# One seed and one gate step per two blocks in a fused attention and expert loop

## The chip, the cores and the metric

The kernel runs on one core of one Trainium2 chip. Its time is the device time of one execution in microseconds (us); the figure for the kernel is the median of several runs. The core has five engines that run side by side, each in the order of its own queue: PE (matrix products and transposes), DVE (vector work), ACT (activation functions, copies), POOL (elementwise work, and the issue of some transfers) and SP (the issue of most transfers). They wait for each other through semaphores.

## What is computed

Two layers on x of 2 x 1024 tokens of width 128 in 32-bit floats. Each layer has two attention-like parts, each followed by a feed-forward part. The change touches the second half of the second layer:

```python
def _L1_attn_b_ref(x, w_qkv, b_qkv, w_proj, b_proj):      # 16 heads of 8
    ...
    dp = jnp.einsum('bhqd,bhkd->bhqk', q, k) * SCALE
    attn = jax.nn.softmax(dp, axis=1)                     # over the heads
    w_avg = jnp.einsum('bhqk,bhkd->bhqd', attn, v)
    ...
    return w_avg @ w_proj + b_proj

def _L1_ffn_ref(hidden_states, Wg, Wu, Wd):               # 8 experts, 128 -> 512 -> 128
    def expert_step(acc, w):
        wg, wu, wd = w
        h = jax.nn.silu(x @ wg) * (x @ wu)
        return (acc + h @ wd, None)
    ...
```

The softmax runs over the 16 heads, not over the keys: for each pair of a query and a key, the exponentials of the 16 scores are divided by their sum. The expert part is applied once before this attention and once after it, so expert work on some tokens can stand beside attention on others.

## The kernel before

The order of all instructions around the change is written out by hand: in `heads_and_experts` each engine gets its instructions in the order in which the Python code records them.

The loop runs over 128 blocks (2 batches x 8 blocks of 128 queries x 8 blocks of 128 keys). One step `i` of it works on several blocks at once, as a pipeline:

- block `i + 1`: `products` (PE, L1237) writes the 16 heads' scores into `h_s`, four banks of PSUM with one buffer. `maxima` (DVE, L1248) takes the maximum over the heads, `exponentials` subtracts it (DVE, L1254) into one of seven `h_e` buffers and applies Exp in two halves (ACT, L1257).
- The sum over 16 heads starts with two transfers: `lower` (SP, L1262) copies heads 0 to 7 into `h_e2`, `upper` (POOL's queue, L1265) adds heads 8 to 15 onto them.
- `denominators` (PE, L1271) adds the remaining 8 by transposes that accumulate in the PSUM tile `h_pd`, which has one buffer. Two blocks share it: even steps and the odd steps after them form a pair. Each pair takes 16 transposes, 8 in a call, where a call has four heads of both blocks.
- In the next even step `inverse` (DVE, L1283) takes the reciprocal of 128 x 256 sums, `turned` (PE, L1288) transposes it back, `evacuated` (ACT, L1292) copies it to `h_r`.
- `normalize` (POOL, L1296) multiplies the block's exponentials by it, four steps after their own; `weigh` (PE, L1301) multiplies by the values one step later. After 8 key blocks the sum is copied (ACT, L1421), its bank set to zero (L1422) and projected (PE, L1383), and `x_res` gets the result (DVE, L1398).

Between these, `ExpertStream` does expert work. A unit is 256 tokens x one expert x 128 of the 512 inner columns. `products` (L1060) makes the gate and up products of a unit in one bank, `e_pgu`, of which there are two; `gates` applies Silu (ACT, L1067), `multiply` multiplies (DVE, L1075), `outputs` makes the Wd products (PE, L1085), at most two units a step. A step takes two units, or one where another use of a bank (`turn` or a side step on PE) comes in. Side steps (`aside`) are the norms and projections of tokens to come. `alone` runs expert work without a block: before the loop until few units are left, and after it for the rest; then `experts_ffn` handles the last 512 tokens.

On ACT, Silu, Exp, Ln and Sqrt need tables; the build puts a load (ACT_TABLE_LOAD) before an activation whose table is not the one that was loaded last. In the loop each step has Silu first and then the next block's Exp.

Of the kernel before, what the change touches and what calls it, by code (L numbers as in the profile page):

```python
# [9 lines left out]
F32 = mybir.dt.float32  # L10
BF16 = mybir.dt.bfloat16
AF = mybir.ActivationFunctionType
ALU = mybir.AluOpType
# [6 lines left out]
P = 128  # L20
# [988 lines left out]
class ExpertStream:  # L1009
# [6 lines left out]

    def __init__(self, g, w, work, ps, sums, zero):
        self.g, self.w, self.work, self.ps, self.sums, self.zero = g, w, work, ps, sums, zero
        self.units, self.fresh, self.gated, self.ready, self.summed, self.done = [], [], [], [], [], []


# [40 lines left out]

    def gates(self):
        nc = self.g.nc
        for chunk, e, fc, pgu in self.fresh:
            sg = self.work.tile([P, 2 * P], F32, name="e_sg", bufs=4)
            nc.scalar.activation(sg, pgu[:, 0, :], AF.Silu)  # L1067
            self.gated.append((chunk, e, fc, pgu, sg))
        self.fresh = []

    def multiply(self):
        nc = self.g.nc
        for chunk, e, fc, pgu, sg in self.gated:
            h = self.work.tile([P, 2 * P], F32, name="e_h", bufs=4)
            nc.vector.tensor_mul(h, sg, pgu[:, 1, :])  # L1075
            self.ready.append((chunk, e, fc, h))
        self.gated = []

    def outputs(self):

# [26 lines left out]
    turned = None  # L1107

    def add(self):

        if self.turned:
            chunk, pt = self.turned
            self.turned = None
            xt = self.tokens(chunk)
            self.g.nc.vector.tensor_add(xt, xt, pt[:, 0:2, :])

# [11 lines left out]
def heads_and_experts(g, w, first, second):  # L1128

    nc, tc = g.nc, g.tc  # L1130
    J, K, HD, H = 4, 4, 8, 16
    scale = HD**-0.5
    with ExitStack() as es:
        pool = lambda name, bufs, **kw: es.enter_context(tc.tile_pool(name=name, bufs=bufs, **kw))
        one = pool("h_one", 1)
        seq = pool("h_seq", 2)
        work = pool("h_work", 2)
        ework = pool("e_work", 2)
        ps_s = pool("h_ps_s", 1, space=PSUM)
        ps_d = pool("h_ps_d", 1, space=PSUM)  # L1140
# [5 lines left out]

        zero = one.tile([P, 1], F32, name="h_zero")
        nc.vector.memset(zero, 0.0)
        held = ps_o.tile([P, 4 * P], F32, name="h_po")
        sums, po, proj = held[:, 0 : 2 * P], held[:, 2 * P : 3 * P], held[:, 3 * P :]  # L1150

# [13 lines left out]
        ex = ExpertStream(g, w, ework, ps_e, sums, zero)  # L1165
# [60 lines left out]
        def spread(b):  # L1226
            v = vs[b].rearrange("p t (j k d) -> p (t j) k d", j=J, k=K)
            for k in range(K):
                nc.scalar.copy(vz[:, :, k, k, :], v[:, :, k, :])
# [34 lines left out]
        def upper(e2, e):  # L1264
            nc.gpsimd.dma_start(out=e2, in_=e[:, 8:16, :], accum_op=ALU.add)  # L1265

        def denominators(pd, pair, half):

            for k in range(4 * half, 4 * half + 4):
                for t in range(2):  # L1270
                    nc.tensor.matmul(  # L1271
                        pd[:, t, :],
                        pair[:, t, k, :],
                        g.ident,
                        start=(k == 0 and t == 0),
                        stop=(k == 7),
                        is_transpose=True,
                        skip_group_check=True,
                    )

        def inverse(pd):
            rT = work.tile([P, 2, P], F32, name="h_rT")
            nc.vector.reciprocal(rT, pd[:, 0:2, :])  # L1283
            return rT

        def turned(pd, rT):
            for t in range(2):
                nc.tensor.transpose(pd[:, 2 + t, :], rT[:, t, :], g.ident)  # L1288

        def evacuated(pd):  # L1290
            r = work.tile([P, 2, P], F32, name="h_r")
            nc.scalar.copy(r, pd[:, 2:4, :])  # L1292
            return r

        def normalize(e, r):
            nc.gpsimd.tensor_mul(e, e, r.unsqueeze(1).to_broadcast([P, H, P]))  # L1296
# [14 lines left out]

        side = [(0, 28 if k else 16, ex.opening(c)) for k, c in enumerate(first[1:])]
        side += [(0, 64, preparation(1, 0))]
        side += [(2 * c + 2, 16 if c else 28, ex.opening(c)) for c in second]
        side.insert(len(first) + 1, (0, 24, preparation(1, 1)))
        finished, current, head, ex.unopened = 0, None, None, len(first)

        def aside(place):  # L1320

            nonlocal current, head
            while True:
                if head is None:
                    if current is None:
                        if not side or side[0][0] > finished or len(ex.units) > side[0][1]:
                            return False
                        current = side.pop(0)[2]
                    head = next(current, None)
                    if head is None:  # L1330
                        current = None
                        continue
                break
            if head[0] != place:
                return False
            step, head = head[1], None
            step()
            return True
# [17 lines left out]
        n = len(blocks)  # L1356
        with tc.manual_schedule(engines=ALL):
            nc.scalar.copy(held, zero.to_broadcast([P, 4 * P]))
            for _, step in ex.opening(first[0]):
                step()  # L1360
            for half in range(2):
                for place, step in preparation(0, half):
                    step()
                    if place != "act":
                        alone()

            while len(ex.units) + 32 * ex.unopened > 76:
                alone()
            spread(0)
            e_, pairs, d_, r_ = {}, {}, {}, {}  # L1370


            oT = resting = None
            for i in range(-1, n + 7):
                now, resting, oT = resting, oT, None
                if i + 1 < n:
                    heads = products(*blocks[i + 1])
                even = i % 2 == 0
                due = even and 0 <= i - 4 < n
                if due:  # L1380
                    rT = inverse(d_[i - 4])
                if now is not None:
                    nc.tensor.matmul(proj, now, w["w_proj2"], start=False, stop=True, skip_group_check=True)  # L1383
                if resting is None:
                    ex.outputs()
                ex.multiply()
                if due:
                    turned(d_[i - 4], rT)
                    r_[i - 4] = evacuated(d_.pop(i - 4))
                ex.products(1 if ex.turn() or aside("pe") else 2)  # L1390
                if resting is not None:
                    ex.outputs()
                if i + 1 < n:
                    m = maxima(heads)
                ex.add()
                if now is not None:
                    xt = g.x[:, finished, :]
                    nc.vector.tensor_add(xt, xt, proj)  # L1398
                    finished += 1
                aside("act")  # L1400
                ex.gates()
                if i + 1 < n:
                    e_[i + 1] = exponentials(heads, m)
                    if not even:
                        pairs[i + 1] = work.tile([P, 2, 8, P], F32, name="h_e2")
                    lower(pairs[i + 1 - even][:, int(even)], e_[i + 1])
                aside("dve")
                pair = i - 2 if even else i - 3
                if not even and 0 <= pair < n:
                    denominators(d_[pair], pairs.pop(pair), 1)  # L1410
                if 0 <= i - 4 < n:
                    normalize(e_[i - 4], r_[i - 4 - i % 2][:, i % 2, :])
                if 0 <= i < n:
                    upper(pairs[i - i % 2][:, i % 2], e_[i])
                aside("pool")
                if 0 <= i - 5 < n:
                    b, qb, kb = blocks[i - 5]
                    weigh(kb, e_.pop(i - 5))
                    if kb == TPB - 1:
                        oT = work.tile([P, P], F32, name="h_oT")  # L1420
                        nc.scalar.copy(oT, po)  # L1421
                        nc.scalar.copy(held[:, 2 * P :], zero.to_broadcast([P, 2 * P]))  # L1422
                        if qb == TPB - 1 and b + 1 < B:
                            spread(b + 1)

                if even and 0 <= pair < n:
                    d_[pair] = ps_d.tile([P, 4, P], F32, name="h_pd")
                    denominators(d_[pair], pairs[pair], 0)
            while ex.busy() or side or current:
                alone()  # L1430

# [221 lines left out]
```

## Time and profile before

| | |
|---|---|
| timed runs (us) | 2206.4, 2212.57, 2213.07; median 2212.57 |
| the profiled execution (us) | 2201.0, its span 2199.3 |
| granted clock of PE, mean | 0.943 |
| busy over the span: PE, DVE, ACT, POOL | 85%, 75%, 60%, 40% |
| first and last maximum of the loop start at (us) | 1186.1 and 2040.4 |
| table loads in the whole span | 372, 1.283 us each |

The profile names each group of instructions by line, engine, operation, and what is written from what; then how many there are, their busy time, the mean of one in ns, and how long the engine stood idle just before them and what ended that. A matrix product in 32-bit floats counts as two instructions in it. The share of busy time is a mean over stages with different limits, so the loop is read by itself, from 1186 to 2047 us; after it come about 152 us of expert work.

### The profile page before, as it was taken

To read this page: it belongs to the slowest core of one execution; us is meant where nothing else is said; L and a number is where in the kernel's file an instruction comes from. 1 tells how busy PE (TensorE), PEld (TensorE's weight loads), DVE (VectorE), ACT (ScalarE), POOL (GpSimd) and SP (SyncE) were. 2 spreads that over 40 slices of the span, in tenths; PEclk is the share of its full clock that TensorE was granted. 3 is DMA by queue.
4 is the path that set the end of the run, shared out by engine and by line. 5 is a ranking of instruction groups with operands and counts; after the bars stand their busy time and mean duration, and the time that the engine had idled before them with its cause. 6 is when DMAs were issued, how large, how long until landed. Compare 5 with 4: busy or idle time off the path is not lost. (4 is left out here: it accounts for less than half of the span.)

```text
span 2199.3 us, 33893 instructions
## 1 busy us (share of the span) xinstructions
PE 1876.8 (85%) x13632; PEld 1068.8 (49%) x13632; DVE 1656.2 (75%) x1955; ACT 1324.5 (60%) x1762; POOL 870.1 (40%) x432
## 2 busy tenths in 40 slices
PE   7669888889967758898688899999888999998999
PEld 4223243333334323334455566666566666666754
DVE  5976867898774699894424989889888989998422
ACT  1026512276633666763544888888888888888422
POOL 0013400063401000000100778777877878887600
PEclk9989979979988979999899999999999999999999
DMA  4000000197623287530001656665655666666200
GB/s 91 1 1 1 1 1 0 49 228 165 157 71 99 57 201 174 136 82 0 1 1 48 154 153 159 155 161 148 160 152 155 165 154 159 168 159 154 68 5 5
DMA packets 73789, 220.01 MB, mean 100 GB/s; under 512 B 9184, under 2 KB 19872, under 8 KB 73504
## 3 DMA queue, kind: packets, MB, share of 16 engines
q1 hardware_dynamic: 54736, 149.40, 23.3%
q0 software_dynamic: 18432, 67.12, 16.0%
q8 instruction: 107, 1.75, 0.3%
q10 hardware_dynamic: 464, 1.33, 0.3%
q14 instruction: 50, 0.41, 0.1%
HBM read 78.35 MB, written 5.24 MB: 38 GB/s over the span
## 5 line engine op out<-in xcount | busy, mean ns | idle before, releaser
L1296 POOL TENSOR_TENSOR h_e<-h_e,h_r 128x2048 f32<-128x2048 f32 x128 | 599.8, 4687 | 109.6 <-issue 100.0
L1248 DVE TENSOR_REDUCE h_m<-h_s 128x128 f32<-128x2048 f32 x128 | 292.7, 2287 | 71.4 <-PE h_s L1237 71.4
L1254 DVE TENSOR_TENSOR h_e<-h_s,h_m 128x2048 f32<-128x2048 f32 x128 | 293.2, 2290 | 9.6 <-DVE h_m L1248 0.4
L1257 ACT ACTIVATE h_e<-h_e 128x1024 f32<-128x1024 f32 x256 | 256.5, 1049 | 23.0 <-DVE h_e L1254 19.4
L1067 ACT ACT_TABLE_LOAD x134 | 171.9, 1283 | 71.6 <-PE e_pgu L1060 70.5
L385 POOL TENSOR_SCALAR_AFFINE_SELECT a_pT<-a_pT 128x256 f32<-128x256 f32 x120 | 128.5, 1092 | 203.2 <-ACT a_pT L382 200.5
L1060 PE MATMUL e_pgu<-e_uT,Wg 128*128 128x256 f32 x640 | 199.8, 395 | 4.4 <-ACT h_qz L1204 2.3
L1075 DVE TENSOR_TENSOR e_h<-e_sg,e_pgu 128x256 f32<-128x256 f32 x320 | 119.6, 402 | 107.7 <-ACT e_sg L1067 103.9
L287 DVE TENSOR_REDUCE a_nm<-a_s 128x2 f32<-128x1024 f32 (+7 forms) x144 | 167.9, 1217 | 38.3 <-PE a_s L278 26.8
L1060 PE MATMUL e_pgu<-e_uT,Wu 128*128 128x256 f32 x640 | 193.8, 385 | 0.0
L1237 PE MATMUL h_s<-h_qz,h_kT 32*128 32x512 f32 x1024 | 153.5, 668 | 46.0 <-DVE h_e L1254 43.2
L1085 PE MATMUL h_po<-e_h,Wd 128*128 128x256 f32 x640 | 188.7, 412 | 4.0 <-DVE e_h L1075 2.3
L1271 PE MATMUL h_pd<-ident,h_e 128*128 128x128 f32 x1024 | 144.9, 279 | 40.8 <-DMA h_e<-h_e 40.7
L1265 POOL DMA_DIRECT2D h_e<-h_e x128 | 119.5, 933 | 140.8 <-DVE h_m L1248 67.7
L382 ACT ACTIVATE a_pT<-a_st 128x1024 f32<-128x1024 f32 (+3 forms) x176 | 129.9, 791 | 65.4 <-PE a_st L368 62.6
L1067 ACT ACTIVATE e_sg<-e_pgu 128x256 f32<-128x256 f32 x320 | 111.5, 382 | 91.6 <-PE e_pgu L1060 76.3
L1257 ACT ACT_TABLE_LOAD x128 | 164.2, 1283 | 2.3
L1085 PEld LDWEIGHTS h_po<-e_h,Wd 128*128 128x128 f32 x640 | 112.8, 196 | 105.6 <-issue 78.9
L800 DVE TENSOR_TENSOR_SCAN s_h<-s_a,s_h 128x1024 f32<-128x1024 f32 x64 | 148.7, 2323 | 17.9 <-ACT s_a L768 14.1
L269 PE MATMUL a_s<-a_latT,a_qT 32*128 32x512 f32 (+3 forms) x768 | 117.0, 583 | 42.0 <-DVE a_nm L287 40.0
L1271 PEld LDWEIGHTS h_pd<-ident,h_e 128*128 128x128 f32 x1024 | 116.7, 142 | 66.7 <-DMA h_e<-h_e 47.0
L1301 PE MATMUL h_po<-h_e,h_vz 128*32 128x128 f32 x4096 | 138.4, 276 | 7.3 <-DVE x_res L1398 6.1
(293 smaller groups left out, 3118.2 us busy)
## 6 DMA issues: line engine op xcount, KB each, us to landing
h_e<-h_e SPq DMA_DIRECT2D x128, 512.0 KB, 4.6
h_e<-h_e POOLq DMA_DIRECT2D x128, 512.0 KB, 5.4
s_a<-s_steps SPq DMA_DIRECT2D x64, 512.0 KB, 5.1
s_h<-s_steps SPq DMA_DIRECT2D x64, 512.0 KB, 6.5
s_steps<-s_gate SPq DMA_DIRECT2D x8, 256.0 KB, 2.0
Wg<-in_Wg_dram SPq DMA_DIRECT2D x8, 256.0 KB, 5.9
Wu<-in_Wu_dram SPq DMA_DIRECT2D x8, 256.0 KB, 5.9
Wd<-in_Wd_dram SPq DMA_DIRECT2D x8, 256.0 KB, 6.0
```

The costliest lines, as they stand in the source:

```text
L287: nc.vector.tensor_reduce(nm[:, half, i, h : h + together], s[:, :, :n], AX.X, ALU.max, negate=True)
L800: nc.vector.tensor_tensor_scan(h, a, h, 0.0, ALU.mult, ALU.add)
L1060: nc.tensor.matmul(pgu[:, k, :], w[name][:, e, f], uT, start=True, stop=True)
L1067: nc.scalar.activation(sg, pgu[:, 0, :], AF.Silu)
L1085: nc.tensor.matmul(self.sums, self.w["Wd"][:, e, fc, :], h, start=False, stop=last, skip_group_check=True)
L1237: nc.tensor.matmul(s[:, j, :].rearrange("p (k q) -> p k q", k=K), kTs[b][quad, bass.ts(kb, P)], qzs[b][qb // 4][quad, :, bass.ts(qb % 4, P ...
L1248: nc.vector.tensor_reduce(m, heads.rearrange("p h q -> p q h"), AX.X, ALU.max)
L1254: nc.vector.tensor_sub(e, heads, m.unsqueeze(1).to_broadcast([P, H, P]))
L1257: nc.scalar.activation(eh, eh, AF.Exp, scale=scale)
L1271: nc.tensor.matmul(pd[:, t, :], pair[:, t, k, :], g.ident, start=(k == 0 and t == 0), stop=(k == 7), is_transpose=True, skip_group_check=True,
L1296: nc.gpsimd.tensor_mul(e, e, r.unsqueeze(1).to_broadcast([P, H, P]))
L1301: nc.tensor.matmul(po[32 * j : 32 * j + 32, :], vz[:, kb * J + j, k].rearrange("p a d -> p (a d)"), a[:, 4 * j + k, :], start=False, stop= ...
```

## The change

The blocks of the loop are taken two at a time in three ways.

- Gates: odd steps make four units' gate products, two units to a bank (`rise`), and apply Silu to a bank at a time (`open_gates`). The even step after them makes the up products into banks of their own (`follow_up`), and the next odd step multiplies (`multiply_pairs`).
- Inverse: in odd steps, behind the second block's transposes, `seed` takes Ln of the sums and Exp of its negative on ACT. In the even step `refined` does one Newton step on DVE, which gives the negated inverse; `evacuated` multiplies by -1 where it copied.
- `denominators` takes one block per call, all 8 heads: the first block in the even step (now ahead of `weigh`), the second in the odd step.

In addition `log_and_exp` applies Ln to one element behind the gates, and a side step that prepares the second batch waits until its tokens' sums are recorded. The core of the diff:

```diff
+    def rise(self, banks):
+        for _ in range(banks):
+            pair, self.units = self.units[:2], self.units[2:]
+            if pair:
+                self.risen.append((pair, self.halves("Wg", pair)))
+    def halves(self, name, pair):
+        pgu = self.ps.tile([P, 4, P], F32, name="e_pgu").rearrange("p (k a) b -> p k (a b)", k=2)
+        for k, (chunk, e, fc, uT) in enumerate(pair):
+            self.g.nc.tensor.matmul(pgu[:, k, :], self.w[name][:, e, bass.ts(fc, P)], uT, start=True, stop=True)
+        return pgu
+    def open_gates(self):
+        for pair, pgu in self.risen:
+            sg = self.work.tile([P, 2, 2 * P], F32, name="e_sg2")
+            self.g.nc.scalar.activation(sg[:, : len(pair)], pgu[:, : len(pair)], AF.Silu)
+            self.opened.append((pair, sg))
+        self.risen = []
+    def follow_up(self):
+        self.paired += [(pair, sg, self.halves("Wu", pair)) for pair, sg in self.opened]
+        self.opened = []
+    def multiply_pairs(self):
+        for pair, sg, pgu in self.paired:
+            h = self.work.tile([P, 2, 2 * P], F32, name="e_h2")
+            self.g.nc.vector.tensor_mul(h[:, : len(pair)], sg[:, : len(pair)], pgu[:, : len(pair)])
...
-        def denominators(pd, pair, half):
-            for k in range(4 * half, 4 * half + 4):
-                for t in range(2):
+        def denominators(pd, pair, t):
+            for k in range(8):
...
-        def inverse(pd):
-            rT = work.tile([P, 2, P], F32, name="h_rT")
-            nc.vector.reciprocal(rT, pd[:, 0:2, :])
+        def seed(pd):
+            rT = work.tile([P, 2, P], F32, name="h_rT", bufs=1)
+            nc.scalar.activation(rT, pd[:, 0:2, :], AF.Ln)
+            nc.scalar.activation(rT, rT, AF.Exp, scale=-1.0)
             return rT
+        def refined(pd, rT):
+            t = work.tile([P, 2, P], F32, name="h_t", bufs=1)
+            nc.vector.tensor_mul(t, rT, pd[:, 0:2, :])
+            nc.vector.scalar_tensor_tensor(rT, t, 2.0, rT, ALU.subtract, ALU.mult)
...
-            nc.scalar.copy(r, pd[:, 2:4, :])
+            nc.scalar.mul(r, pd[:, 2:4, :], -1.0)
...
+        def log_and_exp():
+            nc.scalar.activation(spare, ones, AF.Ln)
...
-                if due:
-                    rT = inverse(d_[i - 4])
+                if not even:
+                    ex.multiply_pairs()
+                pair = i - 4 if even else i - 3
+                due = 0 <= pair < n
+                if due and even:
+                    refined(d_[pair], s_[pair])
+                    turned(d_[pair], s_.pop(pair))
+                    r_[pair] = evacuated(d_.pop(pair))
+                elif due:
+                    denominators(d_[pair], pairs.pop(pair), 1)
+                    s_[pair] = seed(d_[pair])
...
-                ex.multiply()
-                if due:
-                    turned(d_[i - 4], rT)
-                    r_[i - 4] = evacuated(d_.pop(i - 4))
-                ex.products(1 if ex.turn() or aside("pe") else 2)
+                if not even:
+                    ex.rise(1 if ex.turn() or aside("pe") else 2)
+                else:
+                    if len(ex.opened) < 2 and not ex.turn():
+                        aside("pe")
+                    ex.follow_up()
...
-                ex.gates()
+                if not even:
+                    ex.open_gates()
+                    log_and_exp()
...
                 aside("pool")
+                if even and 0 <= i - 2 < n:
+                    d_[i - 2] = ps_d.tile([P, 4, P], F32, name="h_pd")
+                    denominators(d_[i - 2], pairs[i - 2], 0)
                 if 0 <= i - 5 < n:
                     b, qb, kb = blocks[i - 5]
                     weigh(kb, e_.pop(i - 5))
```

In `alone`, the steps `gates` and `multiply` keep one instruction per unit and write two units into one tile.

More of the change, by code (lines that the diff above doesn't have):

```diff
@@ L1018, in __init__ @@
         self.g, self.w, self.work, self.ps, self.sums, self.zero = g, w, work, ps, sums, zero
+        self.risen, self.opened, self.paired, self.added = [], [], [], set()
         self.units, self.fresh, self.gated, self.ready, self.summed, self.done = [], [], [], [], [], []
@@ L1064, in gates @@
         nc = self.g.nc
[L1065 to L1068, printed above, removed]
+        if self.fresh:
+            two = self.work.tile([P, 2, 2 * P], F32, name="e_sg2")
+            for k, (chunk, e, fc, pgu) in enumerate(self.fresh):
+                nc.scalar.activation(two[:, k, :], pgu[:, 0, :], AF.Silu)
+                self.gated.append((chunk, e, fc, pgu, two[:, k, :]))
         self.fresh = []
@@ L1072, in multiply @@
         nc = self.g.nc
[L1073 to L1076, printed above, removed]
-        self.gated = []
+        if self.gated:
+            two = self.work.tile([P, 2, 2 * P], F32, name="e_h2")
+            for k, (chunk, e, fc, pgu, sg) in enumerate(self.gated):
+                nc.vector.tensor_mul(two[:, k, :], sg, pgu[:, 1, :])
+                self.ready.append((chunk, e, fc, two[:, k, :]))
+        self.gated = []
+    def rise(self, banks):
[21 more added lines that the diff above has]
+            self.g.nc.vector.tensor_mul(h[:, : len(pair)], sg[:, : len(pair)], pgu[:, : len(pair)])
+            self.ready += [(chunk, e, fc, h[:, k, :]) for k, (chunk, e, fc, uT) in enumerate(pair)]
+        self.paired = []
     def outputs(self):
@@ L1113, in add @@
             self.turned = None
+            self.added.add(chunk)
             xt = self.tokens(chunk)
@@ L1148, in heads_and_experts @@
         nc.vector.memset(zero, 0.0)
+        ones = one.tile([P, 1], F32, name="h_ones")
+        nc.vector.memset(ones, 1.0)
+        spare = one.tile([P, 1], F32, name="h_spare")
         held = ps_o.tile([P, 4 * P], F32, name="h_po")
@@ L1265, in upper @@
             nc.gpsimd.dma_start(out=e2, in_=e[:, 8:16, :], accum_op=ALU.add)
-        def denominators(pd, pair, half):
-            for k in range(4 * half, 4 * half + 4):
-                for t in range(2):
[L1271 to L1279, printed above, removed]
-        def inverse(pd):
-            rT = work.tile([P, 2, P], F32, name="h_rT")
-            nc.vector.reciprocal(rT, pd[:, 0:2, :])
-            return rT
+        def denominators(pd, pair, t):
+            for k in range(8):
+                nc.tensor.matmul(
+                    pd[:, t, :],
+                    pair[:, t, k, :],
+                    g.ident,
+                    start=(t == 0 and k == 0),
+                    stop=(k == 7),
+                    is_transpose=True,
+                    skip_group_check=True,
+                )
+        def seed(pd):
+            rT = work.tile([P, 2, P], F32, name="h_rT", bufs=1)
+            nc.scalar.activation(rT, pd[:, 0:2, :], AF.Ln)
+            nc.scalar.activation(rT, rT, AF.Exp, scale=-1.0)
+            return rT
+        def refined(pd, rT):
+            t = work.tile([P, 2, P], F32, name="h_t", bufs=1)
+            nc.vector.tensor_mul(t, rT, pd[:, 0:2, :])
+            nc.vector.scalar_tensor_tensor(rT, t, 2.0, rT, ALU.subtract, ALU.mult)
         def turned(pd, rT):
@@ L1308, in weigh @@
                     )
[L1314 to L1317, printed above, removed]
+        side = [(0, 28 if k else 16, ex.opening(c), ()) for k, c in enumerate(first[1:])]
+        side += [(0, 64, preparation(1, 0), first[:2])]
+        side += [(2 * c + 2, 16 if c else 28, ex.opening(c), ()) for c in second]
+        side.insert(len(first) + 1, (0, 24, preparation(1, 1), first[2:]))
         finished, current, head, ex.unopened = 0, None, None, len(first)
@@ L1326, in aside @@
                         if not side or side[0][0] > finished or len(ex.units) > side[0][1]:
+                            return False
+                        if not ex.added.issuperset(side[0][3]):
                             return False
@@ L1369, in heads_and_experts @@
             spread(0)
-            e_, pairs, d_, r_ = {}, {}, {}, {}
+            e_, pairs, d_, r_, s_ = {}, {}, {}, {}, {}
             oT = resting = None
@@ L1375, in heads_and_experts @@
                 now, resting, oT = resting, oT, None
+                even = i % 2 == 0
                 if i + 1 < n:
                     heads = products(*blocks[i + 1])
-                even = i % 2 == 0
-                due = even and 0 <= i - 4 < n
-                if due:
-                    rT = inverse(d_[i - 4])
+                if not even:
[9 more added lines that the diff above has]
+                    s_[pair] = seed(d_[pair])
                 if now is not None:
@@ L1407, in heads_and_experts @@
                 aside("dve")
-                pair = i - 2 if even else i - 3
-                if not even and 0 <= pair < n:
-                    denominators(d_[pair], pairs.pop(pair), 1)
                 if 0 <= i - 4 < n:
@@ L1424, in heads_and_experts @@
                             spread(b + 1)
-                if even and 0 <= pair < n:
-                    d_[pair] = ps_d.tile([P, 4, P], F32, name="h_pd")
-                    denominators(d_[pair], pairs[pair], 0)
+            ex.follow_up()
+            ex.multiply_pairs()
             while ex.busy() or side or current:
```

## The prediction

> **What bounds the kernel now.** I read the stretches of 100 us first, then the groups by form from 850 us on, then the timeline of two blocks, because the diff touches only the loop over 128 blocks. That loop's maximum (L1248) runs from 1186.1 to 2040.4 us: 854.3 us for 127 blocks, 6.73 us each, 13.45 us for a period of two blocks. The stretch below (length, busy PE, PEld, DVE, ACT, POOL, granted clock, DMA share, GB/s) shows a full clock and no engine with much room, DVE with the least.
>
> ```profile
> 1600.00:1700.00 100.00, 87.07 (x896) 62.06 (x895) 90.01 (x76) 85.25 (x111) 79.47 (x29) 1.00 0.61 157
> ```
>
> The groups give the durations; ACT pays two table loads per block.
>
> ```profile
> L1296 POOL TENSOR_TENSOR h_e<-h_e,h_r 128x2048 f32<-128x2048 f32 x128 | 599.8, 4687 | 109.6 <-issue 100.0 <-ACT h_r L1292 9.6
> ...
> L1248 DVE TENSOR_REDUCE h_m<-h_s 128x128 f32<-128x2048 f32 x128 | 292.7, 2287 | 71.4 <-PE h_s L1237 71.4
> L1257 ACT ACTIVATE h_e<-h_e 128x1024 f32<-128x1024 f32 x256 | 256.5, 1049 | 23.0 <-DVE h_e L1254 19.4
> ...
> L1067 ACT ACT_TABLE_LOAD x134 | 171.9, 1283 | 71.6 <-PE e_pgu L1060 70.5
> L1257 ACT ACT_TABLE_LOAD x128 | 164.2, 1283 | 2.3
> ...
> L1283 DVE RECIPROCAL h_rT<-h_pd 128x256 f32<-128x256 f32 x64 | 111.7, 1746 | 10.4 <-PE h_pd L1271 10.4
> ...
> L1292 ACT COPY h_r<-h_pd 128x256 f32<-128x256 f32 x64 | 23.7, 370 | 23.4 <-PE h_pd L1288 22.1
> ```
>
> The timeline shows what sets the period (start, length, engine, line).
>
> ```profile
> 1602.84 2.29 DVE L1254 TENSOR_TENSOR h_e<-h_s,h_m 128x2048 f32<-128x2048 f32 x1
> ...
> 1605.18 1.14 PE L1237 MATMUL h_s<-h_qz,h_kT 32*128 32x512 f32 x8 [0.57 <-DVE h_e L1254]
> ...
> 1606.39 2.29 DVE L1248 TENSOR_REDUCE h_m<-h_s 128x128 f32<-128x2048 f32 x1 [0.61 <-PE h_s L1237]
> ...
> 1608.77 2.29 DVE L1254 TENSOR_TENSOR h_e<-h_s,h_m 128x2048 f32<-128x2048 f32 x1
> ...
> 1610.00 1.28 ACT L1067 ACT_TABLE_LOAD   x1
> 1610.10 0.84 PEld L1301 LDWEIGHTS h_po<-h_e,h_vz 128*32 128x32 f32 x32 [0.35 <-issue]
> ...
> 1610.98 1.75 DVE L1283 RECIPROCAL h_rT<-h_pd 128x256 f32<-128x256 f32 x1
> 1611.18 0.34 PEld L1237 LDWEIGHTS h_s<-h_qz,h_kT 32*128 32x128 f32 x8 [0.24 <-issue]
> ...
> 1611.29 0.66 ACT L1067 ACTIVATE e_sg<-e_pgu 128x256 f32<-128x256 f32 x2
> ...
> 1612.64 0.69 DVE L1075 TENSOR_TENSOR e_h<-e_sg,e_pgu 128x256 f32<-128x256 f32 x2
> ...
> 1613.25 2.28 DVE L1248 TENSOR_REDUCE h_m<-h_s 128x128 f32<-128x2048 f32 x1
> ...
> 1615.64 2.28 DVE L1254 TENSOR_TENSOR h_e<-h_s,h_m 128x2048 f32<-128x2048 f32 x1
> ```
>
> The scores have one buffer, so they are rewritten only when the subtraction has read them: maximum and subtraction 4.67 us (1606.39 to 1611.06), scores 1.21 us from their start to the next maximum. That ring is about 5.95 us a block. In even steps the reciprocal and the multiplications (1.75 + 0.69) outlast the scores, so the period is 4.67 + 1.3 + 4.67 + 2.2 = 12.8, as seen (1602.84 to 1615.64). The other 0.65 of 13.45 are norms, residual adds and waits for DMAs.
>
> **DVE.** Out goes the reciprocal, 1.75. In come a multiplication, 0.40 (L1075, same shape, PSUM operand), and a scalar_tensor_tensor that has no row of this shape: between 0.35 (the shorter of its neighbours) and 0.69 (L574, 128x512); I take 0.40, as it has half those elements. Four multiplications (0.69 + 0.74) become two of 128x512, 0.68 each by L971. So 3.2 becomes 2.2 per period, and both parts nearly fit under the scores: DVE's ring becomes 2 x 5.97 = 11.95. Alone that is -0.85 x 63.5 periods = -54 us.
>
> **ACT.** The built program's list of instructions shows five table loads per period: Ln, Exp of the seed, Silu, the one-element Ln, Exp of the block; so log_and_exp does not do what its name says. Between the first and the last block's exponentials there are 330 loads instead of 263. The old trace has the same habit: all 8 Ln (L716) follow a load, and an Exp after one follows another (L714, L768).
>
> ```profile
> L716 ACT ACT_TABLE_LOAD  x8: 1283/1283/1283, 371.1 to 813.9; - x8
> L716 ACT ACTIVATE s_ln<-s_v x4: 629/630/631, 372.4 to 749.9; 128x512 f32<-128x512 f32 x4
> ```
>
> A load and its successor stand 1.29 apart (1610.00 and 1611.29). Before, a period was 4 x 1.29 + 2 x 2.00 (the halves of a block's Exp overlap: 2.00 a block) + 2 x 0.66 + 0.37 = 10.9, in a period of 12.8: covered. Now it is 5 x 1.29 + 4.00 + two Silu of 128x512 1.10 (0.597 each by L966, overlapping) + Ln, Exp and negated copy of 128x256, 3 x 0.37 + the one-element Ln 0.25 (L66 with 2 elements: 0.30; at least 0.05) = 12.9. Ln lies between 0.37 (L1292's shape) and 0.63 (L716, twice the size); I take 0.37. So ACT alone passes DVE's ring by 0.95.
>
> In the Trainium skill, ScalarE: Activation LUTs, section "Table sets: the hidden batching unit", says Ln then Exp needs one load, since one set holds both. By it three of five loads fall, ACT needs 9.0 and DVE's ring decides; the rows of L716 say otherwise here. The same page, "What ACT_TABLE_LOAD costs", adds a drain of about 1.38 us to each switch: by it the period below would be an estimated 6.9 longer; the 1.29 above shows no such drain.
>
> **The new wait.** In an even step PE's queue holds: scores, the seed's two transposes, Wd products, four Wu products, the first block's 8 denominator transposes, the weighted sum. Those 8 need the one h_pd buffer, so they wait for ACT's negated copy, which in ACT's queue stands behind the odd block's whole Exp. Queued behind them: the weighted sum, the next scores, and the second block's 8 transposes, for which the next Ln waits. So a ring closes. From the copy's end: 0.05, transposes 0.96 (1621.36 to 1622.32, L1271 to L1301), weighted sum 1.08 (1610.13 to 1611.21), scores 1.07 (1618.23 to 1619.30, L1237 to L1085), transposes 1.04, 0.04: Ln starts at 4.24. Meanwhile ACT has done a block's Exp and the Ln load, 3.3: it stalls 0.95. Then Ln 0.37, load 1.29, Exp 0.37, load 1.30, Silu 1.10, load 1.30, small Ln 0.25, load 1.29, block's Exp 2.00, copy 0.39 = 9.66. The period is 13.9.
>
> Covers: scores start 2.1 after the copy, so the subtractions end at 8.0 and 14.0; the first is needed at 11.5, the second only for an Exp whose end Ln awaits with 0.95 to spare. The refinement (0.8) hides under the second scores; bare it would cost 51 us over the loop. POOL keeps its 128 multiplications and 128 DMA issues, 2 x (4.69 + 0.93) = 11.2, and SP its 128 transfers, now behind ACT's later Exp; from the copy, multiplication, issue, multiplication, landing 5.4 after issue make 15.7, while the 8 transposes that need it come at 13.9 + 3.2. If that slipped by 1 us, the ring would grow by 1. PE needs 4 units x 3 products x 0.43 (L1060, 1600.68 to 1601.11) + 2 x (1.07 + 0.96 + 1.05) + 0.4 = 11.7.
>
> **Side work.** Norms and their loads on ACT in the loop: 17 loads x 1.29, e_u and h_u 10.7, h_qz 6.2, copies and roots about 23: 62 us. Half falls in even steps, where the stall covers most; with 15 fewer pair Silu (0.5 each) I take 32 us, 0.5 per period, in place of 0.65. **Tail:** the list has 14 to 46 half-units there for 36 before: Wg 42 for 36, Wu 46, Wd 48 for 40, 24 more products x 0.43 = 10 us on a PE that is 90% busy; bounds 5 to 18 with the longer last chain. I take 11. The stretch before the loop keeps its 52 units, and the tiles of two units hold what four held: nothing. The new condition on the second batch's preparation moves side steps between blocks and issues nothing.
>
> **Sum.** 63.5 x (13.9 + 0.5 - 13.45) = +60, +11: 2201.0 + 71 = 2272 in the profiled execution (span 2199.3). The three timed runs lie 5 to 12 us above it (median 2212.57); I add 8: 2280.
>
> **Rivals.**
> 1. ACT's own sum alone: Ln finds its transposes done. For it: 0.95 of stall is small against my spacings. Against: PE's order is fixed. 12.9 + 0.65 gives 63.5 x 0.1 + 11: 2226.
> 2. All side work on the ring, 62 / 63.5 = 1.0, and the transfers late by 0.3: 15.2, +111 + 11: 2331. POOL's spare 2 us speak against it.
> 3. Faster: one set serves Ln and Exp, so the seed's Exp and the block's Exp pay no load. It decides from one load fewer in the ring on (12.6 + 0.5 is under 13.45); with both gone the ring is 11.3 and DVE's 11.95 decides, 0.2 for multiplications that outlast the scores and 0.65: 12.8, so 63.5 x -0.65 + 11 = -30: 2179. The list and L716 are against it.
> 4. DVE's gain and ACT's loss cancel: 2212.
>
> **How the numbers follow.** Forecast 0.60 (own range 2250 to 2306), rivals 0.20, 0.12, 0.04, 0.04. The range 2224 to 2308 takes in rival 1 and leaves 2 to 4. A change of under 0.3% (7 us) can't be told from none. Faster 0.04 (rival 3), same 0.04 (rival 4), slower 0.92.
>
> **What would show it.** Right: some 450 loads in all (372 before); ACT above 93% in the loop; the subtraction's pairs 14.4 apart; PE idle before h_pd's transposes on ACT h_r; ACT idle before Ln on PE h_pd. Wrong: Exp after Ln without a load, ACT idle on DVE, DVE still the engine without gaps, or a tail past 170 us (152 now).

## The result, and the profile after

| | before | after |
|---|---|---|
| timed runs, median (range), us | 2212.11 (2206.4 to 2213.07) | 2302.56 (2299.15 to 2310.26) |
| span of the profiled execution, us | 2199.3 | 2304.0 |
| first and last maximum of the loop start at, us | 1186.1 and 2040.4 | 1192.1 and 2126.9 |
| the loop, us (per period of two blocks) | 854.3 (13.45) | 934.8 (14.72) |
| behind the last maximum, us | 158.9 | 177.1 |
| table loads in the span | 372 | 450 |

The ratio is 1.0419, 95% interval 1.0385 to 1.0454: slower. Of the 104.7 us that the span grew, 80.5 are the loop, 18.2 the stretch behind it, 6.0 the stretch ahead of it.

The stretch that was shown before, in the kernel after (same columns). ACT has taken DVE's place as the engine with the least room; PE and POOL do less per microsecond.

```profile
1600.00:1700.00 100.00, 77.63 (x828) 54.17 (x826) 84.35 (x60) 90.53 (x111) 74.43 (x28) 1.00 0.57 146
```

The groups by form of the kernel after, from 1180 to 2170 us (the lines have moved: scores are L1275, the maximum is L1286, the subtraction L1292, the blocks' Exp L1295, the denominators' transposes L1308, the copy L1336, the multiplication on POOL L1343, the weighted sum L1348):

```profile
L1295 ACT ACTIVATE h_e<-h_e 128x1024 f32<-128x1024 f32 x256 | 256.4, 1049 | 39.0 <-DVE h_e L1292 38.0
...
L1308 PE MATMUL h_pd<-ident,h_e 128*128 128x128 f32 x1024 | 148.4, 291 | 97.9 <-ACT h_r L1336 97.7 <-DMA h_e<-h_e 0.2
...
L1328 DVE SCALAR_TENSOR_TENSOR h_rT<-h_t,h_rT 128x256 f32<-128x256 f32 x64 | 98.8, 1543 | 2.2
L1295 ACT ACT_TABLE_LOAD x72 | 92.4, 1283 | 1.3
...
L1340 ACT ACT_TABLE_LOAD x67 | 86.0, 1283 | 1.2
L1098 ACT ACT_TABLE_LOAD x67 | 86.0, 1283 | 2.4 <-DVE e_h L1109 1.3
...
L1321 ACT ACT_TABLE_LOAD x64 | 82.1, 1283 | 1.2
L1320 ACT ACT_TABLE_LOAD x63 | 80.8, 1283 | 1.1
...
L1320 ACT ACTIVATE h_rT<-h_pd 128x256 f32<-128x256 f32 x64 | 24.6, 384 | 36.4 <-PE h_pd L1308 35.6
```

Five groups of loads with a count near 64 are the five loads per period. The first block's transposes (L1308) wait 97.7 us for ACT's negated copy, as the prediction had it. Two lines don't fit it. The scalar_tensor_tensor (L1328) takes 1.54 us, not 0.40. And ACT's idle time is split: 35.6 us before Ln, on PE, and 38.0 before the blocks' Exp, on DVE.

The timeline of one period without side work, in the kernel after (start, length, engine, line):

```profile
1449.19 2.04 DVE L1328 SCALAR_TENSOR_TENSOR h_rT<-h_t,h_rT 128x256 f32<-128x256 f32 x1
...
1451.15 2.28 DVE L1286 TENSOR_REDUCE h_m<-h_s 128x128 f32<-128x2048 f32 x1
...
1453.52 2.29 DVE L1292 TENSOR_TENSOR h_e<-h_s,h_m 128x2048 f32<-128x2048 f32 x1
...
1454.51 0.36 ACT L1336 ACTIVATE h_r<-h_pd 128x256 f32<-128x256 f32 x1
...
1454.93 1.09 PE L1308 MATMUL h_pd<-ident,h_e 128*128 128x128 f32 x8 [0.61 <-ACT h_r L1336]
1455.02 4.56 POOL L1343 TENSOR_TENSOR h_e<-h_e,h_r 128x2048 f32<-128x2048 f32 x1 [3.24 <-issue]
...
1455.85 2.01 ACT L1295 ACTIVATE h_e<-h_e 128x1024 f32<-128x1024 f32 x2 [0.97 <-DVE h_e L1292]
...
1455.95 1.08 PE L1348 MATMUL h_po<-h_e,h_vz 128*32 128x128 f32 x32
...
1456.96 1.14 PE L1275 MATMUL h_s<-h_qz,h_kT 32*128 32x512 f32 x8
1457.87 1.28 ACT L1320 ACT_TABLE_LOAD   x1
...
1458.03 1.09 PE L1308 MATMUL h_pd<-ident,h_e 128*128 128x128 f32 x8
...
1459.17 0.38 ACT L1320 ACTIVATE h_rT<-h_pd 128x256 f32<-128x256 f32 x1
...
1460.14 4.81 POOL L1343 TENSOR_TENSOR h_e<-h_e,h_r 128x2048 f32<-128x2048 f32 x1
...
1463.20 2.04 DVE L1328 SCALAR_TENSOR_TENSOR h_rT<-h_t,h_rT 128x256 f32<-128x256 f32 x1
...
1468.41 0.36 ACT L1336 ACTIVATE h_r<-h_pd 128x256 f32<-128x256 f32 x1
```

Read from one copy (L1336) to the next. It ends at 1454.87; the transposes start 0.06 later, then come weighted sum, scores and the second transposes; Ln starts at 1459.17, 4.30 after the copy's end, and the next copy ends at 1468.77, 9.60 after that. Together 13.90: the predicted ring.

Now L1328. POOL's second multiplication runs from 1460.14 to 1464.95. The L1328 that starts inside it, at 1463.20, ends at 1465.24, 0.29 later. Of the 64, 59 start while POOL multiplies, and each ends 0.28 to 0.30 after that multiplication does; the other 5, one of which starts in a multiplication's last 0.1 us, take 0.42 to 0.43. So it doesn't compute for 1.54 us, it is held. The next maximum comes behind it on DVE, then the subtraction, then on ACT the Exp, and Ln stands behind that Exp. This makes a second ring: from a copy's end to the end of POOL's second multiplication 10.1, L1328 0.29, maximum and subtraction 4.66, Exp and load 3.3, which reaches an Ln at 18.3; and 9.60 to a copy. That copy is not the next but the one after it: 27.9 for two periods, 13.95 for one. The two rings come out nearly equal, so the profile alone can't say which one sets the time.

### The profile page after: what moved, and what is told of

Its sections match the earlier page's. It is cut to its first block, busy times and chain, and to the rows that moved or that the text cites. A ratio compares the mean times of both kernels' runs of the same rounds, so it can differ in the third digit from the quotient of the medians.

```text
span 2304.0 us, 34055 instructions
## 1 busy us (share of the span) xinstructions
PE 1883.3 (82%) x13632; PEld 1076.6 (47%) x13632; DVE 1668.1 (72%) x1900; ACT 1467.6 (64%) x1916; POOL 868.3 (38%) x432
## 3 DMA queue, kind: packets, MB, share of 16 engines
q8 instruction: 107, 1.75, 0.3%
## 5 line engine op out<-in xcount | busy, mean ns | idle before, releaser
L1343 POOL TENSOR_TENSOR h_e<-h_e,h_r 128x2048 f32<-128x2048 f32 x128 | 599.2, 4682 | 255.0 <-issue 232.3
L1286 DVE TENSOR_REDUCE h_m<-h_s 128x128 f32<-128x2048 f32 x128 | 292.6, 2286 | 129.5 <-PE h_s L1275 129.4
L1292 DVE TENSOR_TENSOR h_e<-h_s,h_m 128x2048 f32<-128x2048 f32 x128 | 293.1, 2290 | 9.2
L1295 ACT ACTIVATE h_e<-h_e 128x1024 f32<-128x1024 f32 x256 | 256.4, 1049 | 39.0 <-DVE h_e L1292 38.0
L1308 PE MATMUL h_pd<-ident,h_e 128*128 128x128 f32 x1024 | 148.4, 291 | 97.9 <-ACT h_r L1336 97.7
L1308 PEld LDWEIGHTS h_pd<-ident,h_e 128*128 128x128 f32 x1024 | 117.0, 147 | 173.5 <-ACT h_r L1336 121.4
L1119 PE MATMUL h_po<-e_h,Wd 128*128 128x256 f32 x640 | 176.3, 396 | 4.5 <-DVE e_h L1078 2.5
L1275 PE MATMUL h_s<-h_qz,h_kT 32*128 32x512 f32 x1024 | 152.3, 663 | 33.0 <-DVE h_e L1292 33.0
L1303 POOL DMA_DIRECT2D h_e<-h_e x128 | 130.5, 1019 | 83.9 <-DMA h_e<-h_e 71.6
L1348 PE MATMUL h_po<-h_e,h_vz 128*32 128x128 f32 x4096 | 149.2, 290 | 0.5 <-ACT h_po L1125 0.5
L966 ACT ACTIVATE e_sg<-e_pg 128x512 f32<-128x512 f32 x96 | 57.3, 597 | 125.5 <-PE e_pg L963 105.2
L359 PE MATMUL a_st<-a_qT,a_latT 32*128 32x512 f32 (+3 forms) x768 | 122.1, 565 | 10.7 <-ACT a_pT L382 7.2
L1348 PEld LDWEIGHTS h_po<-h_e,h_vz 128*32 128x32 f32 x4096 | 111.9, 115 | 36.2 <-issue 34.9
L971 DVE TENSOR_TENSOR e_h<-e_sg,e_pu 128x512 f32<-128x512 f32 x96 | 64.6, 684 | 83.3 <-PE e_pu L964 71.4
L964 PE MATMUL e_pu<-e_uT,Wu 128*128 128x512 f32 x192 | 102.8, 618 | 20.3 <-DVE e_h L971 20.3
L1092 PE MATMUL e_pgu<-e_uT,Wu 128*128 128x256 f32 x480 | 117.8, 387 | 0.5 <-ACT e_sg L1098 0.4
```

What stands on the lines that cost most here:

```text
L1119: nc.tensor.matmul(self.sums, self.w["Wd"][:, e, fc, :], h, start=False, stop=last, skip_group_check=True)
L1275: nc.tensor.matmul(s[:, j, :].rearrange("p (k q) -> p k q", k=K), kTs[b][quad, bass.ts(kb, P)], qzs[b][qb // 4][quad, :, bass.ts(qb % 4, P ...
L1286: nc.vector.tensor_reduce(m, heads.rearrange("p h q -> p q h"), AX.X, ALU.max)
L1292: nc.vector.tensor_sub(e, heads, m.unsqueeze(1).to_broadcast([P, H, P]))
L1295: nc.scalar.activation(eh, eh, AF.Exp, scale=scale)
L1308: nc.tensor.matmul(pd[:, t, :], pair[:, t, k, :], g.ident, start=(t == 0 and k == 0), stop=(k == 7), is_transpose=True, skip_group_check=True,
```

## The experiments

In the tables below the loop runs from the first to the last maximum; a "plain" period is the lower quartile of the 63 distances between negated copies, so one without side work; the rest is what is left of the span behind the last maximum. Where short and long distances alternate, the lower quartile shows the short ones alone; there the text goes by the lower quartile of two distances in a row, halved (13.99 after). All but the timed ratio come from the profiled execution. For comparison: before 13.45 per period, plain 12.81, rest 158.9; after 14.72, plain 13.90, rest 177.1.

**t into PSUM.** The Newton step's intermediate goes to the half of `h_pd` that the transposes overwrite next, so L1328 has one operand in PSUM.

```diff
-            t = work.tile([P, 2, P], F32, name="h_t", bufs=1)
+            t = pd[:, 2:4, :]
```

> The refinement's product t lies in the free half of h_pd (PSUM) instead of SBUF; nothing else changes. Two theories. Coupled rings: in the changed kernel a plain period is held at 13.9 us twice over, by the wait of the first block's transposes for ACT's copy (4.30 + 9.60 = 13.90) and by the scalar_tensor_tensor that lasts until POOL's multiplication ends (18.31 + 9.60 for two periods = 13.95 each); then the second operation falls from a median of 1.90 us to about 0.42 and the time moves by -15 to 0 us from 2302.6. Rival, the stretched operation is itself what costs: 59 of them 1.2 us too long, about -70 us. If the length does not come from POOL, it stays near 1.9.

Median 2313.11 us, ratio 1.0469 (1.0447 to 1.0491); per period 14.82, plain 13.91, rest 177.8. The groups of this kernel:

```profile
L1308 PE MATMUL h_pd<-ident,h_e 128*128 128x128 f32 x1024 | 152.8, 296 | 142.9 <-ACT h_r L1336 142.2 <-DMA h_e<-h_e 0.7
...
L1328 DVE SCALAR_TENSOR_TENSOR h_rT<-h_pd,h_rT 128x256 f32<-128x256 f32 x64 | 27.1, 424 | 2.2
...
L1320 ACT ACTIVATE h_rT<-h_pd 128x256 f32<-128x256 f32 x64 | 24.6, 385 | 61.9 <-PE h_pd L1308 61.2
```

L1328 is 0.42 now, always, and nothing but the place of one operand was changed: it was held by POOL. The rival's gain of 70 us is not there (the median is 11 us higher, not 0 to 15 lower), and the plain period hasn't moved: the ring through the transposes holds it alone. Most of ACT's idle time is before Ln now, 61.2 / 64 = 0.96 per period, where the prediction had 0.95; the wait before the blocks' Exp fell from 38.0 to 12.6 us. Of the 7.8 us by which this profiled execution is longer than the change's, some 6 lie in periods with side work (57.5 us above plain over the loop, 51.6 in the change); why they grew stayed open.

**Another order of the transposes.** The first block's 8 transposes move into the next odd step, right ahead of the second's, so that weighted sum and scores no longer stand behind the wait for ACT's copy.

```diff
                 elif due:
+                    d_[pair] = ps_d.tile([P, 4, P], F32, name="h_pd")
+                    denominators(d_[pair], pairs[pair], 0)
                     denominators(d_[pair], pairs.pop(pair), 1)
...
-                if even and 0 <= i - 2 < n:
-                    d_[i - 2] = ps_d.tile([P, 4, P], F32, name="h_pd")
-                    denominators(d_[i - 2], pairs[i - 2], 0)
```

> The first block's 8 transposes are moved from the even step to the next odd step, right ahead of the second block's 8, so that ACT's copy no longer holds the weighted sum and the next scores in PE's queue. Coupled rings: the other ring stays at 13.95, so -10 to +10 us from 2302.6, and PE's idle time before the transposes on ACT falls to near nothing. The prediction's ring alone: a plain period falls from 13.9 to ACT's own 12.9, -60 us.

Median 2301.0, ratio 1.0413 (1.0387 to 1.0439); per period 14.63, plain 13.17, rest 179.0. The groups of this kernel:

```profile
L1328 DVE SCALAR_TENSOR_TENSOR h_rT<-h_t,h_rT 128x256 f32<-128x256 f32 x64 | 156.9, 2451 | 2.2
...
L1308 PE MATMUL h_pd<-ident,h_e 128*128 128x128 f32 x1024 | 128.7, 280 | 4.6 <-ACT h_r L1336 4.6
```

As expected, PE's wait for ACT's copy is gone, 97.7 to 4.6 us, and the time is the same within what can be told: L1328 meets POOL's multiplication earlier and is held longer, 2.45 us on the mean. The plain 13.17 is not a shorter period: short and long distances alternate here (13.7, 14.3, 13.7, 14.2 in a row), and of the 62 sums of two in a row only 2 are under 27.85, the lowest tenth 27.91. The second ring, which closes over two periods, had 27.9. One ring opened, the other one stands.

**Both.**

> Both of the two edits before. Coupled rings: -45 to -65 us from 2302.6 (plain period to ACT's own 12.9 to 13.1), although each alone gives nearly nothing. If the effects simply add, it is the sum of the two others.

Median 2257.85, ratio 1.0215 (1.019 to 1.0241); per period 13.97, plain 12.82, rest 179.7. At the edge of what was expected (-45 to -65), and not the sum of the two: neither edit gains anything that can be told alone, together they gain 45 us: two rings of the same length, in parallel. A stretch of the loop, and a part of ACT's timeline (ACT alone; at the mark eight rows are left out):

```profile
1500.00:1600.00 100.00, 82.11 (x845) 57.06 (x844) 82.24 (x78) 98.26 (x122) 72.60 (x28) 0.98 0.57 145
```

```profile
1430.31 1.28 ACT L1320 ACT_TABLE_LOAD   x1
1431.60 0.38 ACT L1320 ACTIVATE h_rT<-h_pd 128x256 f32<-128x256 f32 x1
1432.00 1.28 ACT L1321 ACT_TABLE_LOAD   x1
1433.30 0.42 ACT L1321 ACTIVATE h_rT<-h_rT 128x256 f32<-128x256 f32 x1
...
1443.13 1.28 ACT L1320 ACT_TABLE_LOAD   x1
```

Load to load 12.82 with no gap: this is ACT's own sum, which the prediction put at 12.9. With both rings open ACT is the bound: 98% busy in this stretch, 95% from 1300 to 1800 us.

**One set for Ln and Exp.** In `log_and_exp`, a load of the table set that holds both functions is issued explicitly, so that the build finds both present up to the next Silu.

```diff
         def log_and_exp():
+            nc.scalar.add_instruction(
+                mybir.InstLoadActFuncSet(name=nc.get_next_instruction_name(), engine=ENG.Activation, act_func_set_id=6, ins=[], outs=[])
+            )
             nc.scalar.activation(spare, ones, AF.Ln)
```

> log_and_exp first loads, by an instruction of its own, the table set that holds both Ln and Exp; five table loads per period become two. Table loads as the main cost: Ln to copy falls from 9.60 to 7.1 and ACT's own sum to about 9.1; the ring through PE becomes 11.4, the one through POOL and the refinement 12.05, DVE's 11.95, so a plain period of 12.0 to 12.3 and a time of 2302.6 - 115 = 2187, from 2170 to 2205, faster than before. Rival, loads matter little beside the lock and the queue wait: above 2270.

Median 2187.99, ratio 0.9903 (0.9882 to 0.9925); per period 12.90, plain 11.99, rest 178.8. As expected. There are 275 loads in the span instead of 450; all but 8 periods have two, and in those 8 a norm's root (L66) brings in its own table. ACT's timeline in this kernel:

```profile
1437.68 0.38 ACT L1320 ACTIVATE h_rT<-h_pd 128x256 f32<-128x256 f32 x1
1438.09 0.42 ACT L1321 ACTIVATE h_rT<-h_rT 128x256 f32<-128x256 f32 x1
1438.53 1.28 ACT L1098 ACT_TABLE_LOAD   x1
1439.82 1.08 ACT L1098 ACTIVATE e_sg<-e_pgu 128x512 f32<-128x512 f32 x2
1440.92 1.28 ACT L1340 ACT_TABLE_LOAD   x1
1442.22 0.20 ACT L1343 ACTIVATE h_spare<-h_ones 128x1 f32<-128x1 f32 x1
1442.33 1.99 ACT L1295 ACTIVATE h_e<-h_e 128x1024 f32<-128x1024 f32 x2
```

Ln and the seed's Exp run without a load ahead of them, and the block's Exp too: the load at 1440.92 is the explicit one. Here `log_and_exp` does what its name says, and the change's sign turns: 115 us between five loads a period and two. The plain 11.99 is near DVE's ring, for which the prediction had 11.95; but L1328 is still held here, 1.04 us on the mean, and delays the next maximum in about half of the periods, by some 20 us in all, so this run doesn't part DVE's ring from the one through POOL (12.05 expected).

**No one-element Ln.** The call of `log_and_exp` is left out; the loads per period fall from five to four.

> log_and_exp is left out: the odd step goes from Silu straight to the block's Exp, four table loads per period instead of five. Coupled rings: 1.28 + 0.20 less between Ln and the copy, 9.60 becomes 8.1; the ring through PE becomes 12.4, that through POOL and the refinement (18.31 + 8.1) / 2 = 13.2, so a plain period of 13.2 and 2302.6 - 46 = 2257 (2245 to 2268). Table loads one by one (63 x 1.49 = 94 us): 2209.

Median 2235.53, ratio 1.0120 (1.0077 to 1.0163); per period 13.66, plain 12.75, rest 176.4. Between the two expectations. The distances alternate here too; two in a row, halved, have a lower quartile of 13.21, just the 13.2 of the coupled rings: one load and a one-element Ln, 1.49 us by the trace, took 0.78 off it, which is about half, as a ring that passes them once in two periods should lose. The median is 21 us under the 2257 that the rings had. In the profiled executions it is 28; 6 of them lie ahead of the loop and some 18 in side work: the loop's mean is 0.45 above those 13.21, where in the change it is 0.73 above 13.99. As the program stands after the change, `log_and_exp` only costs.

**Reciprocal.** The change without its inverse: `reciprocal` on DVE where the Newton step was, a plain copy, no Ln, no seed's Exp, no `log_and_exp`. The gate steps and the order of the transposes stay.

```diff
-            nc.scalar.activation(rT, pd[:, 0:2, :], AF.Ln)
-            nc.scalar.activation(rT, rT, AF.Exp, scale=-1.0)
...
-            nc.vector.tensor_mul(t, rT, pd[:, 0:2, :])
-            nc.vector.scalar_tensor_tensor(rT, t, 2.0, rT, ALU.subtract, ALU.mult)
+            nc.vector.reciprocal(rT, pd[:, 0:2, :])
...
-                    log_and_exp()
```

> The inverse alone is undone: DVE's reciprocal in the even step in place of Ln, Exp and the Newton step, a plain copy in place of the negated one, no log_and_exp; gates and transposes stay as changed. Two table loads per period. Rings: ACT no longer holds anything; DVE's ring is 4.67 + 1.75 + 0.05 + 4.67 + 1.3 = 12.45, so 2302.6 - 95 = 2208 (2193 to 2220), about the time before. If the gates of four units and the new order of transposes are at fault too, it stays above 2240.

Median 2171.12, ratio 0.9816 (0.9769 to 0.9863); per period 12.67, plain 12.06, rest 173.1. Better than expected (2193 to 2220). DVE's timeline in this kernel shows why the reciprocal costs less than its 1.75:

```profile
1445.71 1.27 DVE L1109 TENSOR_TENSOR e_h<-e_sg,e_pgu 128x512 f32<-128x512 f32 x2
1447.59 2.29 DVE L1286 TENSOR_REDUCE h_m<-h_s 128x128 f32<-128x2048 f32 x1 [0.61 <-PE h_s L1275]
1449.97 2.29 DVE L1292 TENSOR_TENSOR h_e<-h_s,h_m 128x2048 f32<-128x2048 f32 x1
1452.18 1.75 DVE L1323 RECIPROCAL h_rT<-h_pd 128x256 f32<-128x256 f32 x1
```

It starts as a subtraction ends and runs while PE writes the next scores, which take 1.2; and it is no longer followed by multiplications, which have the other block's scores for cover. So it lengthens the ring by some 0.5. The rest of the change, gate steps and order of transposes above all, is worth 41 us of gain; the inverse by logarithm, with its five loads, then loses 131.

**One set, both edits.**

> Two table loads, with the transposes of both blocks in the odd step and the product t in PSUM. All of the waits named are gone, so DVE's ring (2 x 5.97 = 11.95) and PE's 11.7 remain: a plain period near 11.95, hardly less than with two loads alone (12.0); the periods behind side steps gain a little: 2188 - 10 = 2178 (2168 to 2190). If the lock and the queue wait still cost something of their own: below 2160.

Median 2193.87 (2182.9 to 2195.8), ratio 0.9911 (0.9886 to 0.9937); per period 12.89, plain 12.60, rest 177.7. Less than expected (2168 to 2190): no gain over one set alone. The trace shows a third ring, which the order of the transposes makes on PE. From one block's scores (L1275, start 1404.89) PE goes without a pause through all 16 transposes, Wd products, gate products and the weighted sum to the next block's scores (1411.46), 6.57 us, though the subtraction that frees their buffer had ended at 1410.76; from there to the next scores (1417.49) it is 6.03. Together 12.60, the plain period. With one set alone, where 8 of the transposes stand in the even step, the first stretch takes 6.03. So this kernel trades one wait for another, and it doesn't show what t alone would gain with two loads; that was not run.

**Full odd steps.** The kernel of the last run, with four units' gate products in every odd step, also where a bank serves a side step as well.

```diff
-                    ex.rise(1 if ex.turn() or aside("pe") else 2)
+                    ex.turn() or aside("pe")
+                    ex.rise(2)
```

> As the one before, and an odd step takes four units even where a side step or a turn uses a bank. 22 units (66 products x 0.43 = 28 us of PE) move from the stretch behind the loop into it; there PE has 0.25 us a period to spare, more in the periods with side steps. If the 18 us that the change lost behind the loop are these products: 15 to 28 us less behind the loop, 5 to 15 more in it, net -15 (2150 to 2175). If they are a matter of the last chain of waits: no gain.

Median 2162.34, ratio 0.9789 (0.9751 to 0.9828); per period 13.05, rest 139.1. Within 2150 to 2175, as expected. Behind the last maximum there are 70 products of expert work instead of 136: 66 fewer save 38.6 us there, 0.58 each and more than the 15 to 28 expected, and cost 10 in the loop.

**Reciprocal with full odd steps, and one set with full odd steps** (the change's order and its t).

> Reciprocal on DVE as in the kernel before (no Ln, no seed's Exp, no Newton step, no one-element Ln), the change's order of gates and ups kept, and odd steps that always make four units' gate products. If the tail's length hangs only on the number of expert units left over and the loop has room on PE, the gain found for full steps adds to that of the reciprocal: 2171 - 39 (tail 173 to about 135) + 10 (loop 804 to 814) = 2142, range 2135 to 2152. Rival: the loop with the reciprocal has no room, the 66 products that move into it cost their 0.43 us each there (28 us) and the ends meet at 2160 or above.

> The change with one table set for Ln and Exp (two loads per period) and odd steps that always make four units' gate products; the transposes and the intermediate t stay as the change has them. Theory: t and the place of the transposes cost nothing once the loads are gone, so the time is that of the same kernel with both edits (2162), or lower by the 6 us by which those edits were worse: 2156 to 2164. Rival: the multiplication on POOL holds the refinement up again when PE has more to do, 2170 or more.

| | median us (range) | ratio (95%) | per period | rest |
|---|---|---|---|---|
| reciprocal, full odd steps | 2150.45 (2143.38 to 2155.3) | 0.9748 (0.9712 to 0.9783) | 12.87 | 138.1 |
| one set, full odd steps | 2156.73 (2153.79 to 2157.59) | 0.9776 (0.9753 to 0.9799) | 12.96 | 138.2 |

Both came within the expected ranges and beat both kernels; their intervals overlap. The second, with the change's t and order, is not slower than the kernel with both edits (2162.34): with two loads the two edits together gain nothing. With the reciprocal the loop grew by 12.7 us and the rest fell by 35; from 1600 to 1700 us PE is busy for 94% and DVE for 95%, so little room is left in the loop.

## Why the prediction was right, and where its sizes were off

The sign and the mechanism were right; the forecast, 2280, was 22.6 us short. In the profiled execution 71 us were forecast and 104.7 measured. Step by step:

- **Five loads, no drain: right.** 450 loads. By the Trainium skill, ScalarE: Activation LUTs, "Table sets: the hidden batching unit", Ln and Exp need one load. The run with one set shows that the set is there and serves both; the build did not choose it. The step that mattered, whether the build does choose it, the prediction took from the list of instructions and from L716, and that held.
- **The new wait, 13.9: right.** Measured 13.90 in the change, and 13.91 with the other ring taken out. The stall of 0.95 before Ln showed as 0.96 there. In the change itself 35.6 of these 61.2 us are left before Ln, and the wait before the blocks' Exp is 38.0 instead of 12.6.
- **"Scalar_tensor_tensor 0.40, bounds 0.35 to 0.69": mis-sized.** It needs 0.42 but took 1.54, as it is held until POOL's multiplication ends. This cost the change nothing that can be seen (t in PSUM gains nothing alone), since the ring that it makes, 13.95, is hardly longer than the predicted one, 13.90. That the two are so close is luck: the prediction didn't have the second ring, which alone holds 2301 us when the first is open. It decides once that one is open: 43 us between the second and the third run. So "the refinement hides under the second scores" was true only in its effect: DVE stood idle for 129 us before the maximum, and had room for it.
- **Side work 0.5 per period: mis-sized, some +20 us.** Measured 14.72 - 13.90 = 0.82. The prediction let a stall of 0.95 cover half of the side work. But side work doesn't come evenly: 25 of the 63 distances are more than 1 us above plain, by 2.1 on the mean, and hold 52.8 us together; before, 19 held 32.2. A slack of one microsecond in each period covers little of pieces of two. That the stall covered little is also shown by the run with t in PSUM, where it was there in full and the excess was 57.5.
- **The tail, 11: mis-sized, +7.** Its 24 more products were counted rightly, their price was not: 0.58 each by the run with full odd steps, against 0.43, makes an estimated 14. The other 4 us seem to lie in the drain of the pipeline, by the windows behind the last maximum in the kernel after (same columns; the two first have POOL and DMA work of the last blocks):

```profile
2126.00:2146.00 20.00, 13.66 (x116) 11.16 (x117) 9.46 (x10) 16.88 (x22) 12.57 (x7) 0.83 0.46 115
2146.00:2166.00 20.00, 17.89 (x191) 14.05 (x190) 5.69 (x6) 10.28 (x14) 17.74 (x4) 0.91 0.10 19
2166.00:2186.00 20.00, 19.22 (x117) 16.22 (x117) 7.33 (x21) 11.07 (x20) 0.00 (x0) 1.00 0.00 1
```

  PE is busy 13.66 of the first 20 us, and the granted clock is 0.83; it is 1.00 from the first of these windows on in the kernel before, where PE is busy 17.89 of 20.
- **The stretch before the loop, nothing: off by 6.0.** The kernels with the change have the same program up to the loop, and in their traces it starts between 1186.2 (no one-element Ln) and 1197.6 (full odd steps); before it starts at 1186.1. Most of the difference is already there in the first layer, which the diff doesn't touch (L916 starts last at 1067.8 before, 1073.3 after, 1068.0 without the one-element Ln). So 6.0 is within the spread from one execution to the next and isn't shown to come from the change.
- **8 us between profiled run and median:** there were none. The profiled run of the change, 2305.68, is 3.1 above its median. That took back 11 of the 33.7 by which the sum was short, by luck.

**Rivals.** ACT's own sum alone is what the third run measures: its 12.82 was right (12.9), but at 13.97 per period it has 1.15 of side work and not 0.65, so 2258 instead of 2226. Rival 2 had the side work nearer (1.0) and its late transfers wrong: PE waited 0.2 us for them in the whole loop of the change. Rival 3, one set, is the fourth run: 2187.99, and 12.90 per period where it had 12.8. The chance it got was about whether the build does it, and the build doesn't.

Of the marks set in advance, ACT "above 93%" was met in one of nine stretches from 1200 to 2100 us and missed in the others (90.5 in the one shown, 90.8 on the mean), the distance of 14.4 was 14.72, and the tail from the last exponential's end, 152 before, was 168, short of the 170 that would have spoken against it. Of the marks against the prediction one did show, ACT idle on DVE (38 us), and it pointed to the second ring.

## What to carry to other kernels

Where two waits of the same length close two rings, taking away either shows nothing; an edit that gains nothing alone is refuted only when it has been run with the other's edit too. Work that stands on an engine with a slack of one microsecond per period isn't covered by it if it comes in pieces of two. And before a function is moved to ACT, count the table loads that the build puts around it: here the same arithmetic is 4% slower or 1% faster than before by the set that is loaded, and the plain reciprocal on DVE, started under the score products, is faster still.

## What the runs showed of the hardware

The one instruction of DVE in this loop's inverse with both inputs in SBUF doesn't run beside POOL's multiplication: 59 of 64 ended 0.28 to 0.30 us after it. With one input in PSUM the same instruction took 0.424 on the mean and 0.425 at most, and the subtraction L1292 (one input in PSUM) kept its 2.29 beside POOL all along. The Trainium skill has this: SBUF — State Buffer, "SBUF: two separate sides", tells of a pair of ports which a DVE instruction with two inputs in SBUF and a GpSimd instruction that reads SBUF can't share: the one that starts first holds it to its end, and the other waits. The runs agree where POOL is first, which is the case seen here, and the prediction had missed it.

A load and the next instruction of ACT stand 1.29 apart in every kernel run here where nothing else holds that instruction, 1.283 of it the load. One explicit load of a set that holds two functions was enough for the build to put no other before either, up to the next Silu or root.
